# Queries of layer 2's first token group made tile by tile, PSUM banks handed out earlier, and layer 3 put two expert tiles later

## The chip, the core and the metric

The kernel runs on one core of a Trainium2 chip. A core has five engines with a queue of instructions each, and each queue runs in its own order: TensorE (PE; its weight loads are shown apart as PEld), VectorE (DVE), ScalarE (ACT), GpSimd (POOL) and SyncE (SP, which only issues transfers here). The metric is the device time of one execution in microseconds (us), lower is better: 1113.98 us is the median of three runs of the kernel before (1112.86 to 1116.61).

## What is computed

Four layers work on 2048 tokens of width 256 (8 sequences of 256), with a context of 77 rows per sequence. Each layer is a gated cross attention to the context and a gated feed-forward part:

```python
x = x + tanh(g_xattn[i]) * xattn_i(layernorm(x), ctx)
x = x + tanh(g_ffn[i])   * ffn_i(layernorm(x))
```

- Layer 0: attention of 16 heads with exponential features; a product with a sign matrix.
- Layer 1: attention of one head; a feed-forward part 256-1024-256 with ternary weights, activations rounded to 8 bits per token, and GELU.
- Layer 2: attention of 16 heads in which each query keeps only the 64 largest of its 77 scores; a mixture of 8 experts (256-1024-256, GELU), two per token, with a capacity per expert.
- Layer 3: attention of one head with layer norms and a small feed-forward part; a product with a sign matrix, scaled and clipped.

## The kernel before

**Tiles.** Tokens lie in 16 tiles of 128 rows, in 4 groups `X[0]` to `X[3]` of 4 tiles. The residual stream stays in SBUF. A library places the instructions: the program is traced in Python, each instruction gets a priority by its place in the trace (`tc.high_priority(AHEAD)` moves a block up by 1000), and the library decides each engine's order at build time by reckoning when inputs are ready. The order is then fixed. Tiles of a pool with the same tag share a number of buffers (PSUM banks for PSUM pools); a tile takes a free buffer when its turn in the trace comes.

**Layer 1, first group (lines 804 to 811).** A pool of 8 banks is cut in two rings: `chain` (5) serves `cross1(0)` (attention, lines 584 to 611) and `ffns1(0)` (the feed-forward part, two tiles in flight, lines 655 to 700), `beside` (3) serves `cross1(1)`, the attention of group 1, as work on the side. Line 698 is where a tile of layer 1 is done.

**Keys and values of layer 2 (lines 813 to 860).** `kT2` (keys, line 845) and `V2` (values, line 860) come from the context and weights alone. They follow `cross1(1)` in the ring `beside`. After that the pool is closed and its banks are opened anew (lines 999 to 1006): `psm` (3), the score tile `psc` (one buffer of two banks) and `ps` (3).

**Selection of layer 2 (lines 1018 to 1111 and 1383 to 1423).** `queries(0)` normalizes all four tiles of group 0 (`normal_act`, lines 229 to 259), transposes them, multiplies by `wq2` and writes `qT2` with two ACT operations (line 1030). `distances(n)` makes one tile's scores in two halves in `psc` (lines 1047 and 1055), takes the maximum of each head (line 1062) and writes the distances from it to `pr2` (line 1067). `select` then runs two rounds over 16 heads, MAX8 (line 1405) and MATCH_REPLACE8 (line 1417), which strike out the 13 smallest scores. `finish(n)` makes weights from the rest (Abs and Exp on ACT, sum at line 1083, POOL's scaling at line 1085), transposes them (1091), multiplies by `V2` (1097), copies to `oT2` (1103) and projects (1107, 1110).

**Order by hand.** Inside `tc.manual_schedule(engines=ordered)` DVE keeps the order of the trace. `select` calls `gap()` after every 8 heads of a round; each call advances the other work by a step: `front` (`groups1`: layer 1 of groups 1 and 2 with the keys and values of the second half, `keys1`, line 561 to 578), `finish`, `route`, and `queries(g)` of later groups. Whatever a step traces for DVE stands there between the rounds.

**Experts and layer 3 (lines 868 to 984, 1445 to the end).** Routed token rows are gathered from `xbuf`, a tile of 128 at a time, with the weights of the expert (`fetch`, lines 914 and 919, POOL), transposed (930), multiplied (943, GELU 947, 955), scaled (960) and scattered into `ybuf` (965). `experts(0)` has 16 tiles for the first half of the tokens, `experts(1)` 25 for the second half, the last three of them only if needed; the first 8 of these also write rows of the first half. Layer 3's `stream(i)` loads two tiles of results (`yg`, line 1559), adds them (1565), normalizes (1522 to 1530), transposes (1539) and goes on in eight steps. The program traces ten tiles of `experts(1)`, then `run(0, 3)` (three streams), the other expert tiles, then `run(3, 8)`.

Of the kernel before, what the change touches and what calls it, by code (L numbers as in the profile page):

```python
# [21 lines left out]
KC = D // P  # L22
NB = 8
SQ = 256
SK = 77
# [33 lines left out]
def flamingo_kernel(ctx: ExitStack, tc: tile.TileContext, io: dict):  # L59
# [741 lines left out]
    a2s = ExitStack()  # L801
    a2 = a2s.enter_context(tc.tile_pool(name="a2", bufs=1, side="right", reuse_waits="tile"))
    a2w = a2s.enter_context(tc.tile_pool(name="a2w", bufs=2, side="right", reuse_waits="tile"))
    with tc.tile_pool(name="a1p", bufs=8, space=PSUM, side="right", reuse_waits="tile") as ps:
        chain, ps = Banks(ps, "chain", 5), Banks(ps, "beside", 3)
        for _ in cross1(0, chain, b1w, *kv1, False):
            pass
        for _ in ffns1(0, chain, b1w, False):
            pass
        for _ in cross1(1, ps, b1w, *kv1, False):  # L810
            pass

        nm = a2.tile([P, NB, SK], BF16, name="nm")
        nmf = nm.rearrange("p b k -> p (b k)")
        nc.vector.tensor_copy(nmf, mask_u8)
        some = a2.tile([P, NB], F32, name="some")  # L820
        nc.vector.tensor_reduce(some, nm, AX.X, ALU.max)
        nc.vector.tensor_scalar(nmf, nmf, 2.0**100, -(2.0**100), ALU.mult, ALU.add)
        onesb = a2.tile([P, P], BF16, name="onesb")
        nc.vector.memset(onesb, 1.0)
        bq4 = a2.tile([P, KC], F32, name="bq4")
        nc.vector.tensor_scalar(bq4, cols[:, C_WQB * KC : (C_WQB + 1) * KC], 0.25, None, ALU.mult)
        wob3 = rows3(a2, V_WOB, "wob")

        kT2 = a2.tile([P, KC, NB, 2, SK], F32, name="kT2")
        V2 = a2.tile([SK, NB, 8, 2, 2, 16], F32, name="V2")
        nc.gpsimd.memset(V2.rearrange("p b r q s d -> p (b r q s d)"), 0.0)

        for hb in range(2):
            for oc in range(KC):
                pk = ps.tile([P, 512], F32, name="pk", tag="ps")
                for kc in range(KC):
                    nc.tensor.matmul(
                        pk[:, :HB], wk2[:, kc, oc * P : (oc + 1) * P],  # L840
                        ctxT[:, kc, hb * HB : (hb + 1) * HB],
                        start=(kc == 0), stop=(kc == KC - 1),
                    )
                for q in range(2):
                    nc.vector.tensor_scalar(
                        kT2[:, oc, 4 * hb : 4 * hb + 4, q, :],
                        pk[:, :HB].rearrange("p (b k) -> p b k", k=SK),
                        col(C_WKB, oc), par[:, q : q + 1], ALU.add, ALU.mult,
                    )
            for b in range(4 * hb, 4 * hb + 4):  # L850
                pv = ps.tile([P, 512], F32, name="pv", tag="ps")
                for kc in range(KC):
                    nc.tensor.matmul(
                        pv[:SK, :D], ctxT[:, kc, b * SK : (b + 1) * SK], wv2[:, kc, :],
                        start=(kc == 0), stop=(kc == KC - 1),
                    )
                pvv = pv[:SK, :D].rearrange("p (r q d) -> p r q d", q=2, d=16)
                bvv = vrow(V_WVB, SK).rearrange("p (r q d) -> p r q d", q=2, d=16)
                for q in range(2):
                    nc.vector.tensor_add(V2[:, b, :, q, q, :], pvv[:, :, q, :], bvv[:, :, q, :])  # L860


    done1 = [0]
# [43 lines left out]
    def experts(h, psm, f2w, widx, tok, gate, row, ahead=0):  # L907
# [88 lines left out]

    psm = ctx.enter_context(tc.tile_pool(name="f2p", bufs=3, space=PSUM, reuse_waits="tile"))
    banks = ExitStack()  # L1000
    psc = banks.enter_context(
        tc.tile_pool(name="a2s", bufs=1, space=PSUM, side="right", reuse_waits="tile")
    )
    ps = banks.enter_context(
        tc.tile_pool(name="a2p", bufs=3, space=PSUM, side="right", reuse_waits="tile")
    )

    ZR = GT
    zero = work.tile([P, ZR * D], F32, name="zero", tag="xn")
# [6 lines left out]
                )  # L1016

    qs = {}

    def queries(g):  # L1020
        _, xT = normal_act(g, ps)
# [51 lines left out]
    def finish(n, pr):  # L1073

        b = n // 2
        g, t = divmod(n, GT)
        prf = pr.rearrange("p j c k -> p (j c k)")
        nc.scalar.activation(prf, prf, AF.Abs, scale=some[:, b : b + 1])
        nc.scalar.activation(prf, prf, AF.Exp, scale=-1.0)
        yield  # L1080
        yield
        sm = small.tile([P, 4, 4], F32, name="sm")
        nc.vector.tensor_reduce(sm, pr, AX.X, ALU.add)
        nc.vector.reciprocal(sm, sm)  # L1084
        nc.gpsimd.tensor_tensor(pr, pr, sm.unsqueeze(3).to_broadcast([P, 4, 4, SK]), ALU.mult)  # L1085
        po = ps.tile([P, KC, P], F32, name="po", tag="ps")
        for c in range(KC):
            for q in range(2):
                pt = ps.tile([P, 4, P], F32, name="pta", tag="ps")
                for j in range(4):  # L1090
                    nc.tensor.transpose(pt[:SK, j, :], pr[:, j, 2 * c + q, :], ident)  # L1091
                aT = a2w.tile([SK, 4, P], F32, name="aT2", bufs=3)
                nc.scalar.copy(  # L1093
                    aT.rearrange("p j n -> p (j n)"), pt[:SK].rearrange("p j n -> p (j n)")
                )
                for j in range(4):
                    nc.tensor.matmul(  # L1097
                        po[32 * j : 32 * j + 32, c, :],
                        V2[:, b, 4 * c + j, q, :, :].rearrange("p s d -> p (s d)"),
                        aT[:, j, :], start=(q == 0), stop=(q == 1),  # L1100
                    )
        oT = a2w.tile([P, KC, P], F32, name="oT2")
        nc.scalar.copy(oT.rearrange("p c n -> p (c n)"), po.rearrange("p c n -> p (c n)"))
# [289 lines left out]
    def select(n0, n1):  # L1393

        with tc.high_priority(AHEAD):
            for pr in distances(n0):
                nxt = pr
        for n in range(n0, n1):
            pr = nxt
            ahead = distances(n + 1) if n + 1 < n1 else iter(())  # L1400
            rows = [pr[:, j, c, :] for j in range(4) for c in range(4)]
            for r in range(2):
                m8 = a2w.tile([P, H, 8], F32, name=f"m8{r}")
                for i, row in enumerate(rows):
                    nc.vector.max(m8[:, i, :], row)  # L1405
                    if i == H - 1:
                        while n + 1 < n1 and (n + 1) // GT not in qs:
                            gap()
                        with tc.high_priority(AHEAD):
                            nxt = next(ahead, None)  # L1410
                    if i % 8 == 7:
                        gap()
                if r == 1:

                    nc.vector.memset(m8[:, :, NDROP - 8 :], -BIG)
                for i, row in enumerate(rows):
                    nc.vector.match_replace(row, m8[:, i, :], row, -BIG)  # L1417
# [7 lines left out]

    at = {}
    ordered = {mybir.EngineType.DVE}
    with tc.manual_schedule(engines=ordered):
        with tc.high_priority(AHEAD):
            for _ in queries(0):  # L1430
                pass
        front = groups1(psm, kv1)
        steps.append(front)
        select(0, HT)
        last = steps.pop()
        while steps:
            gap()
# [29 lines left out]
    with tc.tile_pool(name="a3", bufs=1, side="right", reuse_waits="tile") as a3, \  # L1467
# [203 lines left out]


        second = experts(1, psm, f2w, *at[1])
        for _ in range(NE + 2):
            next(second)
        n = NT // SN // 2
        run(0, n - 1, [ps])
# [87 lines left out]
```

## Time and profile before

| what | value |
|---|---|
| median of the runs | 1113.98 us |
| the profiled execution's own time | 1120.5 us |
| its span on the chip | 1118.7 us |
| busy: PE, PEld, DVE, ACT, POOL | 906.9, 669.7, 657.7, 495.5, 307.5 us |
| mean granted PE clock | 0.833 of full |
| from 300 to 540 us: DVE busy | 200.9 of 240 us |
| first MAX8 of the selection | 299.77 us |
| first expert tile's matmuls | near 600 us |

The profile is of one execution; its times are microseconds from the start of the span. A row of the timeline has the start, the length, the engine, the line, the operation with output and inputs, how often, and in brackets the idle time of the engine just before with the instruction that ended it. Busy PE is not PE at its peak, since matmuls are pipelined. An idle engine costs something only where the end waits for it.

### The profile page before, as it was taken

To read this page: it belongs to the slowest core of one execution; us is meant where nothing else is said; L and a number is where in the kernel's file an instruction comes from. 1 tells how busy PE (TensorE), PEld (TensorE's weight loads), DVE (VectorE), ACT (ScalarE), POOL (GpSimd) and SP (SyncE) were. 2 spreads that over 40 slices of the span, in tenths; PEclk is the share of its full clock that TensorE was granted. 3 is DMA by queue.
4 is the path that set the end of the run, shared out by engine and by line. 5 is a ranking of instruction groups with operands and counts; after the bars stand their busy time and mean duration, and the time that the engine had idled before them with its cause. 6 is when DMAs were issued, how large, how long until landed. Compare 5 with 4: busy or idle time off the path is not lost.

```text
span 1118.7 us, 16730 instructions
## 1 busy us (share of the span) xinstructions
PE 906.9 (81%) x5884; PEld 669.7 (60%) x5896; DVE 657.7 (59%) x2849; ACT 495.5 (44%) x1012; POOL 307.5 (27%) x333
## 2 busy tenths in 40 slices
PE   4677898958778688686878898899999688997895
PEld 2455565725444345453556776788999676896663
DVE  4779965658588978887677757715300225201664
ACT  3334444124366556564616765543222165222552
POOL 2352323020110300121004223333344363431530
PEclk9689899959967587665557988999999989998697
DMA  6200000003000000100124443566888861782001
GB/s 217 102 1 3 1 1 1 1 1 150 1 0 1 1 1 1 38 1 1 39 81 170 170 169 106 177 238 230 298 304 310 316 216 44 257 322 102 21 11 38
DMA packets 27179, 115.77 MB, mean 103 GB/s; under 512 B 4324, under 2 KB 16332, under 8 KB 21973
## 3 DMA queue, kind: packets, MB, share of 16 engines
q0 software_dynamic: 9504, 90.71, 22.3%
q1 hardware_dynamic: 17589, 23.96, 6.0%
q8 instruction: 48, 0.79, 0.3%
q14 instruction: 38, 0.31, 0.1%
HBM read 99.19 MB, written 15.47 MB: 102 GB/s over the span
## 4 chain that ended last, share of the span: by engine, by line
PE 39%; DVE 22%; ACT 13%; issue 10%; POOL 10%; DMA 5%; SPq 0%; POOLq 0%; ACTq 0%; DVEq 0%
PE pta L1091 3%; PE phm L943 3%; DVE pr L1417 3%; PE pym L955 3%; DMA ybuf<-yo,row 2%; PE pta L473 2%; ACT pr L1067 2%; PE po L1097 2%; DVE m L1405 2%; PE py L488 2%; POOL ybuf L965 2%; DMA yg<-ybuf 2%; POOL xg L914 1%; POOL pr L1085 1%; PE po L476 1%
## 5 line engine op out<-in xcount | busy, mean ns | idle before, releaser
L943 PE MATMUL phm<-xgT,wt 128*128 128x128 f32 x1216 | 152.6, 280 | 1.2 <-ACT yo L960 0.6
L955 PE MATMUL pym<-wt,hT 128*128 128x256 f32 x608 | 149.6, 391 | 3.1 <-ACT hT L947 3.0
L943 PEld LDWEIGHTS phm<-xgT,wt 128*128 128x128 f32 x1216 | 147.5, 195 | 5.8 <-issue 3.0
L955 PEld LDWEIGHTS pym<-wt,hT 128*128 128x128 f32 x608 | 113.7, 195 | 19.2 <-ACT hT L947 4.8
L1417 DVE MATCH_REPLACE8 pr<-m,pr 128x77 f32<-128x77 f32 x512 | 107.1, 224 | 0.0
L1085 POOL TENSOR_TENSOR pr<-pr,sm 128x1232 f32<-128x1232 f32 x16 | 36.0, 2249 | 186.0 <-DVE sm L1084 166.9
L947 ACT ACTIVATE hT<-phm 128x512 f32<-128x512 f32 x76 | 45.4, 597 | 81.6 <-PE phm L943 72.6
L1405 DVE MAX8 m<-pr 128x8 f32<-128x77 f32 x512 | 77.2, 223 | 0.0
L1091 PE MATMUL pta<-ident,pr 128*77 128x128 f32 x256 | 54.4, 351 | 24.2 <-POOL pr L1085 24.2
L1067 ACT ACTIVATE pr<-sc,mx 128x77 f32<-128x77 f32 x256 | 59.0, 340 | 24.8 <-DVE mx L1062 24.7
L919 POOL DMA_INDIRECT wt<-in_w,widx x38 | 37.3, 981 | 111.9 <-PE pym L955 74.8
L1093 ACT COPY aT<-pta 77x512 f32<-77x512 f32 x64 | 36.7, 589 | 63.9 <-PE pta L1091 63.6
L965 POOL DMA_INDIRECT ybuf<-yo,row x46 | 46.2, 1003 | 67.0 <-ACT yo L960 50.5
L1047 PE MATMUL sc<-kT,qT 32*128 32x154 f32 x256 | 38.6, 406 | 31.1 <-ACT pr L1067 30.9
L1565 DVE TENSOR_TENSOR x<-x,yg 128x512 f32<-128x512 f32 x16 | 12.8, 807 | 86.6 <-DMA yg<-ybuf 86.5
L960 ACT ACTIVATE yo<-pym,gate 128x256 f32<-128x256 f32 x38 | 18.1, 476 | 98.6 <-issue 48.9
L1091 PEld LDWEIGHTS pta<-ident,pr 128*77 128x77 f32 x256 | 37.8, 189 | 38.7 <-POOL pr L1085 26.8
L474 ACT COPY aT<-pta 77x512 f32<-77x512 f32 x64 | 35.5, 581 | 56.4 <-PE pta L473 56.4
L456 POOL TENSOR_TENSOR pr<-pr,sm 128x1232 f32<-128x1232 f32 x16 | 36.8, 2300 | 84.7 <-DVE sm L455 50.1
L914 POOL DMA_INDIRECT xg<-xbuf,tok x38 | 37.5, 986 | 74.2 <-PE ptm L930 50.2
L473 PE MATMUL pta<-ident,pr 128*77 128x128 f32 x256 | 44.8, 319 | 16.0 <-POOL pr L456 9.2
L1047 PEld LDWEIGHTS sc<-kT,qT 32*128 32x128 f32 x256 | 25.1, 239 | 45.4 <-ACT pr L1067 38.3
(387 smaller groups left out, 1944.8 us busy)
## 6 DMA issues: line engine op xcount, KB each, us to landing
ybuf<-zero SPq DMA_DIRECT2D x8, 512.0 KB
yg<-ybuf SPq DMA_DIRECT2D x16, 256.0 KB
xbuf<-xn SPq DMA_DIRECT2D x6, 512.0 KB
x<-in_x SPq DMA_DIRECT2D x4, 512.0 KB
raw_f1w<-in_f1w SPq DMA_DIRECT2D x2, 1024.0 KB
out<-x SPq DMA_DIRECT2D x8, 256.0 KB
vec<-in_vec SPq DMA_DIRECT2D x1, 896.0 KB
ybuf<-yo,row POOLq DMA_INDIRECT x46
```

Of the source, the lines that this page charges most:

```text
L473: nc.tensor.transpose(pt[:SK, j, :], pn2[i][:, j, c, :], ident)
L914: nc.gpsimd.indirect_dma_start(out=xg[:, :], out_offset=None, in_=xbuf[h][:, :], in_offset=bass.IndirectOffsetOnAxis(ap=tok[:, m : m + 1], ...
L943: nc.tensor.matmul(ph[:, i, :], wt[:, kc * FF + fc * P : kc * FF + (fc + 1) * P], xgT[:, kc, :], start=(kc == 0), stop=(kc == KC - 1),)
L947: nc.scalar.activation(hT[:, NFC // 2 * fq : NFC // 2 * (fq + 1), :], ph, AF.Gelu)
L955: nc.tensor.matmul(py, hT[:, fc, :], wt[:, KC * FF + fc * D : KC * FF + (fc + 1) * D], start=(fc == 0), stop=(fc == NFC - 1),)
L965: nc.gpsimd.indirect_dma_start(out=dst[:, :], out_offset=bass.IndirectOffsetOnAxis(ap=row[:, m : m + 1], axis=0), in_=yo[:, :], in_offset= ...
L1047: nc.tensor.matmul(sc[:, jj, c * 2 * SK : (c + 1) * 2 * SK], qT[32 * j : 32 * j + 32, c, t * P : (t + 1) * P], kT2[32 * j : 32 * j + 32, c ...
L1067: nc.scalar.activation(pr[:, j0 + jj, c, :], sc[:, jj, c * SK : (c + 1) * SK], AF.Identity, bias=mx[:, jj, c : c + 1], scale=-1.0,)
L1085: nc.gpsimd.tensor_tensor(pr, pr, sm.unsqueeze(3).to_broadcast([P, 4, 4, SK]), ALU.mult)
L1091: nc.tensor.transpose(pt[:SK, j, :], pr[:, j, 2 * c + q, :], ident)
L1405: nc.vector.max(m8[:, i, :], row)
L1417: nc.vector.match_replace(row, m8[:, i, :], row, -BIG)
```

## The change

Four edits.

1. **Banks.** The pools `psm`, `psc` and `ps` are opened at the start of layer 1, ahead of `cross1(0)`, and the pool of 8 with its two rings is gone. `cross1(0)` and `ffns1(0)` take from `psm` (3 banks), the side work from `ps` (3).
2. **Side work.** The keys `kT2` of both halves now come ahead of `cross1(1)` in the trace; the values `V2` stay behind it.
3. **Queries.** `queries(0)` is replaced by `queries0(t)` for each tile: statistics on DVE, four small operations on POOL, one normalizing ACT operation, two transposes and four matmuls in a tile of `psc`, three more ACT operations. Its two SBUF tiles share the two buffers of `oT2`. Tile 0 is traced ahead of the ordered part, tile 1 ahead of the first round, and tile n+2 behind the first MAX8 of the second round of selection n.
4. **Layer 3.** `run(0, 3)` is traced behind twelve tiles of `experts(1)`, not ten.

```diff
-    with tc.tile_pool(name="a1p", bufs=8, space=PSUM, side="right", reuse_waits="tile") as ps:
-        chain, ps = Banks(ps, "chain", 5), Banks(ps, "beside", 3)
-        for _ in cross1(0, chain, b1w, *kv1, False):
-            pass
-        for _ in ffns1(0, chain, b1w, False):
-            pass
-        for _ in cross1(1, ps, b1w, *kv1, False):
-            pass
+    psm = ctx.enter_context(tc.tile_pool(name="f2p", bufs=3, space=PSUM, reuse_waits="tile"))
+    banks = ExitStack()
+    psc = banks.enter_context(
+        tc.tile_pool(name="a2s", bufs=1, space=PSUM, side="right", reuse_waits="tile")
+    )
+    ps = banks.enter_context(
+        tc.tile_pool(name="a2p", bufs=3, space=PSUM, side="right", reuse_waits="tile")
+    )
+    for _ in cross1(0, psm, b1w, *kv1, False):
+        pass
+    for _ in ffns1(0, psm, b1w, False):
+        pass
...
+    for hb in range(2):
+        for oc in range(KC):
+            pk = ps.tile([P, 512], F32, name="pk", tag="ps")
...
+    for _ in cross1(1, ps, b1w, *kv1, False):
+        pass
+    for b in range(NB):
+        pv = ps.tile([P, 512], F32, name="pv", tag="ps")
...
+    def queries0(t):
+
+        if t == 0:
+            qs[0] = a2w.tile([P, KC, GN], F32, name="qT2")
+        x, rows = X[0][:, t, :], slice(t * P, (t + 1) * P)
+        xn = a2w.tile([P, D], F32, name="xn_q0", tag="oT2")
+        xT = a2w.tile([P, KC, P], F32, name="xT_q0", tag="oT2")
+        st = small.tile([P, 6], F32, name="q0_st")
+        mv = small.tile([P, 2], F32, name="q0_mv")
+        nc.vector.bn_stats(st, x)
+        nc.vector.bn_aggr(mv, st)
+        rs = small.tile([P, 1], F32, name="q0_rs")
+        nc.gpsimd.tensor_scalar(rs, mv[:, 1:2], EPS, None, ALU.add)
+        nc.gpsimd.tensor_tensor(rs, rs, mhalf[:, :1], ALU.pow)
+        m = small.tile([P, 1], F32, name="q0_nm")
+        nc.gpsimd.tensor_tensor(m, mv[:, 0:1], rs, ALU.mult)
+        nc.gpsimd.tensor_scalar(m, m, -1.0, None, ALU.mult)
+        nc.scalar.activation(xn, x, AF.Identity, bias=m, scale=rs)
+
+        two = psc.tile([P, 2, 512], F32, name="sc")
+        pt, pq = two[:, 0, : KC * P], two[:, 1, : KC * P]
+        for kc in range(KC):
+            nc.tensor.transpose(
+                pt[:, kc * P : (kc + 1) * P], xn[:, kc * P : (kc + 1) * P], ident
+            )
+        nc.scalar.copy(xT, pt.rearrange("p (c n) -> p c n", c=KC))
+        for oc in range(KC):
+            for kc in range(KC):
+                nc.tensor.matmul(
+                    pq[:, oc * P : (oc + 1) * P], wq2[:, kc, oc * P : (oc + 1) * P],
+                    xT[:, kc, :], start=(kc == 0), stop=(kc == KC - 1),
+                )
+            nc.scalar.activation(
+                qs[0][:, oc, rows], pq[:, oc * P : (oc + 1) * P], AF.Identity,
+                bias=bq4[:, oc : oc + 1], scale=0.25,
+            )
...
-        oT = a2w.tile([P, KC, P], F32, name="oT2")
+        oT = a2w.tile([P, KC, P], F32, name="oT2", tag="oT2")
...
+            if n == 0:
+                with tc.high_priority(AHEAD):
+                    queries0(1)
             for r in range(2):
                 m8 = a2w.tile([P, H, 8], F32, name=f"m8{r}")
                 for i, row in enumerate(rows):
                     nc.vector.max(m8[:, i, :], row)
+                    if r == 1 and i == 0 and n + 2 < GT:
+                        with tc.high_priority(AHEAD):
+                            queries0(n + 2)
...
+    with tc.high_priority(AHEAD):
+        queries0(0)
     with tc.manual_schedule(engines=ordered):
-        with tc.high_priority(AHEAD):
-            for _ in queries(0):
-                pass
...
-        for _ in range(NE + 2):
+        for _ in range(NE + 4):
             next(second)
```

More of the change, by code (lines that the diff above doesn't have):

```diff
@@ L803, in flamingo_kernel @@
     a2w = a2s.enter_context(tc.tile_pool(name="a2w", bufs=2, side="right", reuse_waits="tile"))
-    with tc.tile_pool(name="a1p", bufs=8, space=PSUM, side="right", reuse_waits="tile") as ps:
-        chain, ps = Banks(ps, "chain", 5), Banks(ps, "beside", 3)
-        for _ in cross1(0, chain, b1w, *kv1, False):
-            pass
-        for _ in ffns1(0, chain, b1w, False):
-            pass
-        for _ in cross1(1, ps, b1w, *kv1, False):
-            pass
[L817 to L860, printed above, removed]
@@ new lines, in flamingo_kernel @@
+    psm = ctx.enter_context(tc.tile_pool(name="f2p", bufs=3, space=PSUM, reuse_waits="tile"))
[10 more added lines that the diff above has]
+        pass
+    nm = a2.tile([P, NB, SK], BF16, name="nm")
@@ new lines, in flamingo_kernel @@
+    nmf = nm.rearrange("p b k -> p (b k)")
+    nc.vector.tensor_copy(nmf, mask_u8)
+    some = a2.tile([P, NB], F32, name="some")
+    nc.vector.tensor_reduce(some, nm, AX.X, ALU.max)
+    nc.vector.tensor_scalar(nmf, nmf, 2.0**100, -(2.0**100), ALU.mult, ALU.add)
+    onesb = a2.tile([P, P], BF16, name="onesb")
+    nc.vector.memset(onesb, 1.0)
+    bq4 = a2.tile([P, KC], F32, name="bq4")
+    nc.vector.tensor_scalar(bq4, cols[:, C_WQB * KC : (C_WQB + 1) * KC], 0.25, None, ALU.mult)
+    wob3 = rows3(a2, V_WOB, "wob")
@@ new lines, in flamingo_kernel @@
+    kT2 = a2.tile([P, KC, NB, 2, SK], F32, name="kT2")
+    V2 = a2.tile([SK, NB, 8, 2, 2, 16], F32, name="V2")
+    nc.gpsimd.memset(V2.rearrange("p b r q s d -> p (b r q s d)"), 0.0)
+    for hb in range(2):
[3 more added lines that the diff above has]
+                nc.tensor.matmul(
+                    pk[:, :HB], wk2[:, kc, oc * P : (oc + 1) * P],
+                    ctxT[:, kc, hb * HB : (hb + 1) * HB],
+                    start=(kc == 0), stop=(kc == KC - 1),
+                )
+            for q in range(2):
+                nc.vector.tensor_scalar(
+                    kT2[:, oc, 4 * hb : 4 * hb + 4, q, :],
+                    pk[:, :HB].rearrange("p (b k) -> p b k", k=SK),
+                    col(C_WKB, oc), par[:, q : q + 1], ALU.add, ALU.mult,
+                )
@@ new lines, in flamingo_kernel @@
+    for _ in cross1(1, ps, b1w, *kv1, False):
[3 more added lines that the diff above has]
+        for kc in range(KC):
+            nc.tensor.matmul(
+                pv[:SK, :D], ctxT[:, kc, b * SK : (b + 1) * SK], wv2[:, kc, :],
+                start=(kc == 0), stop=(kc == KC - 1),
+            )
+        pvv = pv[:SK, :D].rearrange("p (r q d) -> p r q d", q=2, d=16)
+        bvv = vrow(V_WVB, SK).rearrange("p (r q d) -> p r q d", q=2, d=16)
+        for q in range(2):
+            nc.vector.tensor_add(V2[:, b, :, q, q, :], pvv[:, :, q, :], bvv[:, :, q, :])
@@ L986, in experts @@
                     one(m, NM[h])
[L999 to L1006, printed above, removed]
     ZR = GT
@@ L1018, in flamingo_kernel @@
     qs = {}
+    def queries0(t):
[17 more added lines that the diff above has]
+        pt, pq = two[:, 0, : KC * P], two[:, 1, : KC * P]
+        for kc in range(KC):
+            nc.tensor.transpose(
+                pt[:, kc * P : (kc + 1) * P], xn[:, kc * P : (kc + 1) * P], ident
+            )
+        nc.scalar.copy(xT, pt.rearrange("p (c n) -> p c n", c=KC))
+        for oc in range(KC):
+            for kc in range(KC):
+                nc.tensor.matmul(
+                    pq[:, oc * P : (oc + 1) * P], wq2[:, kc, oc * P : (oc + 1) * P],
+                    xT[:, kc, :], start=(kc == 0), stop=(kc == KC - 1),
+                )
+            nc.scalar.activation(
+                qs[0][:, oc, rows], pq[:, oc * P : (oc + 1) * P], AF.Identity,
+                bias=bq4[:, oc : oc + 1], scale=0.25,
+            )
     def queries(g):
```

## Prediction

> **What bounds the kernel now.** I read the table of stretches first, then who waited for whom, then the instructions in order of time at the two places that the change touches. The page's own chain is spread thin (PE 39%, DVE 22%, ACT 13%, issue 10%), so shares do not help: each place has its own limit.
>
> Around 300 us layer 1 hands over to layer 2. Columns: stretch, length, busy us of PE, PEld, DVE, ACT, POOL, then PE clock, DMA share, GB/s.
>
> ```profile
> 236.00:260.00 24.00, 15.07 (x68) 7.64 (x70) 18.98 (x64) 8.01 (x12) 6.07 (x6) 0.66 0.34 139
> 260.00:272.00 12.00, 8.78 (x50) 5.02 (x49) 7.08 (x20) 7.70 (x11) 0.00 (x0) 0.86 0.18 72
> 272.00:288.00 16.00, 15.11 (x81) 10.48 (x80) 13.16 (x40) 4.37 (x8) 1.71 (x4) 1.00 0.01 2
> 288.00:300.00 12.00, 12.00 (x60) 6.72 (x60) 1.75 (x4) 5.05 (x15) 0.00 (x0) 1.00 0.00 0
> ```
>
> From 272 to 300 PE is full (27.1 of 28 us) and DVE, which will carry the selection, does 1.75 us of work in the last 12. The DVE rows say why:
>
> ```profile
> 260.20 0.47 DVE L698 SCALAR_TENSOR_TENSOR x<-pyf,q_dn,x 128x256 f32<-128x256 f32 x1
> ...
> 280.05 0.48 DVE L698 SCALAR_TENSOR_TENSOR x<-pyf,q_dn,x 128x256 f32<-128x256 f32 x1 [0.61 <-PE pyf L693]
> ...
> 294.84 0.80 DVE L1062 TENSOR_REDUCE mx<-sc 128x8 f32<-128x616 f32 x1 [7.06 <-PE sc L1055]
> 299.05 0.80 DVE L1062 TENSOR_REDUCE mx<-sc 128x8 f32<-128x616 f32 x1 [3.41 <-PE sc L1055]
> 299.77 1.21 DVE L1405 MAX8 m<-pr 128x8 f32<-128x77 f32 x8
> 300.90 1.27 DVE L578 TENSOR_TENSOR V<-pv,vec 77x512 f32<-77x512 f32 x2
> ```
>
> Tile 0 of group 0 leaves layer 1 at 260.7, tile 3 at 280.5; the first MAX8 comes at 299.77, because the queries are made for the four tiles at once. Right behind stands L578, layer 1's values for the second half: in the order written for DVE it precedes the rest of the first selection.
>
> From 780 to 885 PE is full with expert tiles, one each 7.24 us (L943 starts at 844.19 and 851.43). There it stops:
>
> ```profile
> 885.42 1.46 PE L955 MATMUL pym<-wt,hT 128*128 128x256 f32 x6
> 887.93 0.69 DVE L1565 TENSOR_TENSOR x<-x,yg 128x512 f32<-128x512 f32 x1 [80.61 <-DMA yg<-ybuf]
> ...
> 898.98 2.08 ACT L1530 ACTIVATE xn<-x,n_nm,n_rs 128x256 f32<-128x256 f32 x4 [12.98 <-DVE n_nm L1528]
> 899.63 1.39 PE L1539 MATMUL pt<-ident,xn 128*128 128x128 f32 x4 [12.75 <-ACT xn L1530]
> 900.82 2.77 PE L955 MATMUL pym<-wt,hT 128*128 128x256 f32 x6
> ```
>
> Layer 3's first transposes stand in PE's order inside the eleventh expert tile (6 of its 16 pym are out), and their input needs the scatters of tile 8, a load and a normalization: PE stands 12.75 us with work behind it.
>
> **Banks and kT2.** Five banks become three for group 0's layer 1. Its tiles take banks in program order: ptx of tile 2 (259.96) follows pyf of tile 0 (259.09) although five are there. Gelu empties a bank in 0.7 us. I take 0, bounds 0 and +3. kT2 now stands ahead of cross1(1) in its ring. Before, its first matmul came at 272.46, just behind the last pyv of cross1(1) (271.75), although PE idled 8.9 us in 236:260. It can now fill 218:236, where PE idles 6.4 us and DVE 11.5: 16 matmuls, 4.6 us of PE (L839), and 8 DVE operations of 0.54 (4.3 us) leave the full stretch. Pushed between the links of cross1(0), each is at most 0.59 long: +1 us, bounds 0 and +2.
>
> **Queries by tile.** One tile's chain: statistics 0.42 + 0.17; POOL four small ones, 1.96 us for four columns (281.37 to 283.33), the power 1.04 of it (0.71 for two columns, L1526), so 1.5; ACT xn 0.59; two transposes 0.4; ACT copy 0.37 (L932); four matmuls 0.9; the last ACT 0.39 (between 0.34 for 77 columns and 0.465 for 256). With hand-overs 6 us, 7 to the first mx. For group 0, eight short query activations replace two of 0.69: ACT +1.7 us, in a stretch where it is 5 to 8 of 12 us busy; at nothing, or 1.7 if that cover goes. Tile 0: 260.7 + 6 = 266.7; from complete queries to the first MAX8 the rows take 5.8 (293.97 to 299.77); with 2 for a crowded ACT, MAX8 at 275. DVE then does eight and waits for L578. That is PE's matter: from 272 to 300 it loses 4.6 (kT2) and 4.7 (queries: eight L1026 at 0.43, transposes 1.2), and gains 1.3 (tile 1), net 8, and values of layer 2 may use the 3.2 us idle in 260:272. L578 comes at 290 to 293: **-10** us, bounds -5 (kT2 alone) and -13.
>
> **What the new waits take back.** The shared score tile has one buffer, and queries0 takes it too. Tile 2's chain stands in DVE's order behind the first MAX8 of the second half; the next mx on it came 2.9 us after that point (314.5 to 317.33). 7 + 0.6 against 2.9: DVE stands 4.5 us, and all select and front work is queued behind that mx. The next idle on DVE, 3.35 at 326.69 waiting for gelu, is then partly over: +2 net, bounds 0 and +4.5. Tile 1's chain costs 1 at most, inside L578's wait. Tile 3's is worse: its two tiles share the two slots of oT2, and in program order oT of tile 0 stands ahead.
>
> ```profile
> 339.26 1.42 DVE L1083 TENSOR_REDUCE sm<-pr 128x16 f32<-128x1232 f32 x1
> 349.74 0.78 DVE L1062 TENSOR_REDUCE mx<-sc 128x8 f32<-128x616 f32 x1
> 356.30 0.41 ACT L1103 COPY oT<-po 128x256 f32<-128x256 f32 x1
> ```
>
> oT came 17.0 us behind sm, the mx 10.5. Now: oT at sm + 15.4 (the 1.8 us of L1067 just ahead of it go behind), then xn to mx, 4.4: mx at sm + 19.8, a stall of 9.3. The idles that follow (1.60, 1.39, 1.22 at 352 to 363) are absorbed: **+5**, bounds 0 and +17. Over the eight tiles sm to oT takes 12.6 to 23.5; the last gives the upper end (23.5 + 4.4 - 10.5). No DMA moves past another one here, and V2's memset and the zeroing keep their cover. Sum of this half: +1 - 10 + 2 + 5 = -2.
>
> **Layer 3 two tiles later.** Ten expert tiles ahead become twelve. PE's place for the transposes moves from 886.9 to behind the rest of the eleventh tile (10 x 0.226 = 2.3) and the twelfth (7.24): 896.4. Their input is ready at 899.6 as before; 3.2 us of 12.75 stay: **-9.5**. Bounds: 0, if the transposes still slip in early; -14, with the whole wait and the 1.4 us of the slow restart (below) gone. POOL changes too: the thirteenth tile's fetches now come ahead of layer 3 in the program. Before, they went out at 896.95 and 900.24, behind n_rs, which waited 9.13 us; if they stay there, PE has after 899.6 only layer 3's serial work until those weights land, and the gain shrinks towards its lower end. The streams end near 960 and twelve tiles of 7.24 followed; with ten left they are still covered, so the tail does not move.
>
> The restart is slow in the rows: six pym take 2.77 us at 900.82 and 1.36 at the pace of the tiles before (16 in 3.62), 1.4 apart, at a PE clock of 0.55 in 899.6:905 and 1.00 after. I count none of it. [...]
>
> **Sum.** -2 - 9.5 = -11.5. The profiled execution took 1120.5 us (span 1118.7, 1.8 around it), 6.5 above the median 1113.98; the differences are carried to the median: 1102.5.
>
> **Rivals.**
> 1. Forecast: start pulled forward, mostly eaten by the query waits; layer 3's wait mostly gone: 1102.5, chance 0.50.
> 2. The waits are absorbed by idle that comes anyway (DVE idles 39 us in 300:540): +1 - 10 - 9.5 = -18.5, 1095.5. For: each later idle waits for ACT or PE, which run on. Against: the select order is serial. 0.15.
> 3. Layer 3 does not move: the planner put the transposes where its own reckoning had the input ready, mid-tile, and may again find a hole there. -2: 1112. 0.17.
> 4. Slower. The oT2 ring: place, the third selection's second mx; price, 17.4 at the longest sm to oT, with 4.5 and 1 before it and nothing absorbed, 23. It decides once the stalls pass the 10 + 9.5 gained, less 1 for kT2. 23 + 1 - 19.5 = +4.5: 1118.5. For: every DVE instruction there is in a written order. Against: with DVE standing, ACT and PE reach oT sooner. 0.15.
>
> The other 0.03 is for causes not listed: 0.01 near no change, 0.02 slower.
>
> **Numbers.** 0.3% is 3.3 us, about what a measurement of this kernel tells from none. Faster: 0.50 + 0.15 + 0.05 of rival 3 = 0.70. Within: its other 0.12 and 0.01, 0.13. Slower: 0.15 and 0.02, 0.17. The range 1091 to 1117 takes in the forecast with its bounds, rival 2 and rival 3, and leaves out most of rival 4.
>
> **What would show it.** Right: first MAX8 near 275; L578 near 291; an idle of some 9 us on DVE ahead of an mx, ended by PE sc, about 20 us after the first sm; kT2 before 236; the L1539 wait down to about 3 and standing behind the twelfth pym. Wrong: L578 still at 300, no idle at those mx, L1539 inside the eleventh tile, or the first expert tile starting as late as now.

## The result, and the profile after

The changed kernel took 1124.1 us (median of 12 runs, 1118.3 to 1126.6) and the one before, beside it, 1117.19 (12 runs, 1112.86 to 1121.1): ratio 1.0057, interval 1.0038 to 1.0075. The forecast of 1102.5 and its range of 1091 to 1117 miss it.

Two later sets gave the same kernel 0.9979 (0.9952 to 1.0005) and 0.9971 (0.9949 to 0.9993). So the sign is not settled; what is settled is that the 11.5 us of the forecast are not there. The profiles say why, if they are cut at five landmarks, A, C, D, E and F (there is no B). All numbers are us; "again" and "third" are profiled executions of the two later sets, one each.

| stretch | before | after | again | third |
|---|---|---|---|---|
| start to A: the last sixteen matmuls of L303 (layer 0) begin | 214.5 | 219.4 | 218.6 | 220.2 |
| A to C: fourth L698 of group 1, layer 1 | 152.8 | 160.4 | 158.8 | 160.5 |
| C to D: first expert matmul | 229.6 | 228.6 | 228.7 | 226.5 |
| D to E: layer 3's first load is issued | 276.9 | 273.0 | 269.2 | 272.4 |
| E to F: last expert scatter | 149.5 | 148.4 | 146.4 | 147.9 |
| F to the end of the span | 95.4 | 94.0 | 94.9 | 94.2 |
| A to the end | 904.2 | 904.4 | 897.9 | 901.5 |

**The first row is not the change's.** The edits begin behind A: on PE, DVE, ACT and POOL both programs run the same instructions in the same order until 5.5 us behind it. Yet of the 20 profiled executions in this study 7 reached A at 213.9 to 214.6 and 13 at 218.3 to 222.3. The table of stretches shows where, before first, then after (same columns as in the prediction):

```profile
75.00:80.00 5.00, 4.33 (x36) 2.48 (x34) 3.79 (x7) 3.36 (x5) 2.25 (x1) 1.00 0.00 0
85.00:90.00 5.00, 3.38 (x36) 2.04 (x35) 4.96 (x6) 1.58 (x3) 0.00 (x0) 1.00 0.06 12
```

```profile
75.00:80.00 5.00, 4.33 (x24) 2.65 (x20) 2.59 (x5) 2.70 (x4) 1.45 (x1) 0.50 0.00 0
85.00:90.00 5.00, 5.00 (x23) 4.06 (x24) 4.56 (x4) 0.00 (x0) 1.09 (x1) 0.50 0.00 0
```

With the same idle of 4.1 us on PE near 68 (4.10 and 4.09) the granted clock falls to half (0.50 from 70 to 75 in both); in one execution it is back at 75, in the other at 90. So 4.9 us must be taken off every later time of the changed kernel's first profile before it is set beside the old one. Below, "A + 56" means 56 us behind A.

**The start.** Stretches of the changed kernel and DVE's rows:

```profile
272.00:288.00 16.00, 13.37 (x91) 8.94 (x93) 11.66 (x37) 8.86 (x27) 2.15 (x4) 0.92 0.01 2
288.00:300.00 12.00, 12.00 (x69) 8.49 (x69) 4.22 (x15) 2.30 (x4) 0.00 (x0) 1.00 0.00 0
```

```profile
265.12 0.47 DVE L698 SCALAR_TENSOR_TENSOR x<-pyf,q_dn,x 128x256 f32<-128x256 f32 x1
...
285.41 1.07 DVE L1443 MAX8 m<-pr 128x8 f32<-128x77 f32 x7
...
290.97 0.48 DVE L698 SCALAR_TENSOR_TENSOR x<-pyf,q_dn,x 128x256 f32<-128x256 f32 x1 [1.28 <-PE pyf L693]
...
299.09 0.69 DVE L578 TENSOR_TENSOR V<-pv,vec 77x512 f32<-77x512 f32 x1 [3.32 <-PE pv L574]
```

PE is full in the last 12 us, as it was. These windows are not moved by the 4.9 us: in the same place behind A (283.09 to 295.09) DVE was busy for 3.95 of 12 us before, so its 4.22 us are hardly more. Tile 0 is done at A + 45.7, as before. The first MAX8 comes at A + 66.0 (before: 85.3), 19 us sooner. But L578, behind which the rest waits, comes at A + 79.7 against 86.4: 6.7 sooner. Tile 3 is done at A + 71.6 against 65.5.

**The two waits.** Below, "mx" is the reduction that takes the maximum of each head (two for each tile), and "sm" the sum in `finish`. The fourth mx came without a wait before:

```profile
317.33 0.78 DVE L1062 TENSOR_REDUCE mx<-sc 128x8 f32<-128x616 f32 x1
```

Now tile 2's queries are made ahead of it. On the engines that they pass through:

```profile
314.00 0.41 DVE L1027 BATCH_NORM_STATS2 q_st<-x 128x6 f32<-128x256 f32 x1
315.64 4.41 PE L592 MATMUL pq<-xT,w_wq 128*128 128x512 f32 x6 [0.46 <-ACT xT L258]
316.31 0.60 ACT L1035 ACTIVATE xn_q<-x,q_nm,q_rs 128x256 f32<-128x256 f32 x1 [0.23 <-POOL q_nm L1034]
319.89 0.38 PE L1040 MATMUL sc<-ident,xn_q 128*128 128x128 f32 x2
325.03 0.80 DVE L1097 TENSOR_REDUCE mx<-sc 128x8 f32<-128x616 f32 x1 [7.72 <-PE sc L1090]
```

The normalized tile is there at 316.9, but PE's order has six matmuls of layer 1's queries in front, and the transposes start at 319.89. PE's granted clock was 0.50 from 313 to 318 us, and the first four of the six start 0.85 to 1.0 us apart, the last two 0.43. Layer 1's matmuls stand between the later steps of the chain too (320.20 to 321.56, 322.00 to 322.85). The mx stands 7.72 us. Tile 3's:

```profile
343.44 1.42 DVE L1118 TENSOR_REDUCE sm<-pr 128x16 f32<-128x1232 f32 x1
347.39 0.41 DVE L1027 BATCH_NORM_STATS2 q_st<-x 128x6 f32<-128x256 f32 x1
357.84 0.38 ACT L1138 COPY oT<-po 128x256 f32<-128x256 f32 x1
358.11 0.61 ACT L1035 ACTIVATE xn_q<-x,q_nm,q_rs 128x256 f32<-128x256 f32 x1
363.08 0.80 DVE L1097 TENSOR_REDUCE mx<-sc 128x8 f32<-128x616 f32 x1 [9.06 <-PE sc L1090]
```

Its statistics are taken at 347.39 and its normalization runs at 358.11, right behind oT, whose ring it shares. The mx comes 19.6 us behind sm and stands 9.06.

**Layer 3.** The issue of the loads (SP), first before, then after, and the root of the first streams before (POOL):

```profile
873.85 11.78 SPq L1559 DMA_DIRECT2D yg<-ybuf  x6
...
898.01 2.06 POOL L1526 TENSOR_TENSOR n_rs<-n_rs,mhalf 128x2 f32<-128x2 f32 x3
```

```profile
881.39 12.64 SPq L1599 DMA_DIRECT2D yg<-ybuf  x6
```

After, the loads as they land (DVE), the root (POOL), and PE:

```profile
904.16 0.69 DVE L1605 TENSOR_TENSOR x<-x,yg 128x512 f32<-128x512 f32 x1 [7.74 <-DMA yg<-ybuf]
907.09 0.23 POOL L1565 TENSOR_SCALAR n_rs<-n_mv 128x2 f32<-128x2 f32 x1
...
918.54 2.06 POOL L1566 TENSOR_TENSOR n_rs<-n_rs,mhalf 128x2 f32<-128x2 f32 x3
...
920.16 1.39 PE L1579 MATMUL pt<-ident,xn 128*128 128x128 f32 x4 [9.89 <-ACT xn L1570]
```

The first stream's additions are done at 904.9 and its epsilon is added at 907.09. But POOL takes its power (the first of the three at 918.54) only behind the epsilon additions of the second and third stream (915.13 and 917.12), and these wait for their own loads. The order was the same before (the three powers in a row from 898.01, behind the last epsilon at 896.58); there the loads landed closer together. PE stands 9.89 us, in the thirteenth tile, with the input 38.8 us behind the loads' issue (881.39) instead of 25.8 (873.85 to 899.63).

### The profile page after: what moved, and what is told of

It is laid out like the page before. It is cut to its first block, busy times and chain, and to the rows that moved or that the text cites. A ratio compares the mean times of both kernels' runs of the same rounds, so it can differ in the third digit from the quotient of the medians.

```text
span 1123.8 us, 16790 instructions
## 1 busy us (share of the span) xinstructions
PE 906.2 (81%) x5907; PEld 670.9 (60%) x5920; DVE 657.1 (58%) x2849; ACT 497.3 (44%) x1020; POOL 310.6 (28%) x345
## 4 chain that ended last, share of the span: by engine, by line
PE 39%; DVE 24%; ACT 12%; POOL 10%; issue 9%; DMA 6%; SPq 1%; POOLq 0%; ACTq 0%; DVEq 0%
PE pta L1126 3%; DVE pr L1458 3%; DMA yg<-ybuf 3%; PE phm L949 3%; PE py L488 2%; DVE m L1443 2%; DMA ybuf<-yo,row 2%; PE po L1132 2%; PE pym L961 2%; PE pta L473 2%; ACT pr L1102 2%; POOL ybuf L971 2%; POOL pr L1120 2%; DVE sm L1118 2%; PE sc L1082 1%
## 5 line engine op out<-in xcount | busy, mean ns | idle before, releaser
L961 PE MATMUL pym<-wt,hT 128*128 128x256 f32 x608 | 146.8, 386 | 3.0 <-ACT hT L953 3.0
L1126 PEld LDWEIGHTS pta<-ident,pr 128*77 128x77 f32 x256 | 37.7, 189 | 39.1 <-POOL pr L1120 26.6
L473 PEld LDWEIGHTS pta<-ident,pr 128*77 128x77 f32 x256 | 33.4, 170 | 31.0 <-issue 12.7
```

Source lines behind the costliest of these rows:

```text
L473: nc.tensor.transpose(pt[:SK, j, :], pn2[i][:, j, c, :], ident)
L961: nc.tensor.matmul(py, hT[:, fc, :], wt[:, KC * FF + fc * D : KC * FF + (fc + 1) * D], start=(fc == 0), stop=(fc == NFC - 1),)
```

## Experiments

Three theories are open. T1: the waits for the queries of tiles 2 and 3 eat the earlier start. T2: layer 3's input came later with the tiles, so its wait moved instead of going. T3, the rival: the loss sits ahead of A and is chance. Ratios are to the runs of before in the same set.

**Each part alone, and the whole again.** Layer 3 alone is the kernel before with

```diff
-        for _ in range(NE + 2):
+        for _ in range(NE + 4):
```

> The kernel before with twelve expert tiles ahead of layer 3 instead of ten, nothing else. Theory A (the loads of layer 3 share the DMA engines with two more tiles' weights, so their input is later too, and PE's wait moves instead of going): PE still waits about 10 us ahead of the first transposes, the yg loads land over some 15 us instead of 6, gain about 3 us, ratio 0.995 to 0.999. Theory B (the term of the prediction: input ready as before, wait down to 3): ratio 0.990 to 0.993. Theory C (the whole loss of the change comes from here): slower, ratio 1.004 or more.

Ratio 0.999 (0.9969 to 1.001), not told apart from no gain. Theory A is right about the place: PE's wait is 6.74 (it had about 10), E to F 144.7 against 149.5. The eight additions of loaded rows run from 887.2 to 912.5 (before: 887.9 to 895.7); the first stream's are done at 889.2, and its power comes at 914.74. The start alone is the changed kernel with NE + 2:

> The changed kernel with ten tiles ahead of layer 3, so the part at the start of layer 2 alone. Theory A (the two query chains that the selection waits for cost more than the earlier start brings): idles on DVE of about 7.7 and 9 us ahead of the mx of the second and third selection; from the last L303 matmuls of layer 0 to the fourth L698 of group 1 about 160 us against 152.8 before; time 5 to 10 us above before, ratio 1.004 to 1.009. Rival (the 4.9 us by which the profiled execution is late already at 215 us are all there is, and they are the changed program's own): the lateness at 215 us comes again, and the stretch behind it costs about nothing. Rival C: the start part is worth nothing and layer 3 loses, ratio 0.999 to 1.001.

Ratio 1.000 (0.9977 to 1.0022); waits 7.69 and 9.06, A to C 160.3. This execution reached A at 214.0 with the changed start: the lateness of 4.9 does not belong to it. Theory A's waits and stretch are there, but not its 1.004 to 1.009; what becomes of the difference is told at the end of the next section.

> The changed kernel itself once more, beside the same runs of before as the other kernels of this set. Since its two parts alone came out at 1.000 and 0.999, theory A (the two parts add up, and the first ratio of 1.0057 held several us of the executions' own scatter, which comes from the clock granted between 70 and 90 us) expects 0.998 to 1.001. Theory B (the two parts together cost something that neither costs alone): 1.004 to 1.008. In either case the stretch from the last L303 matmuls to the fourth L698 of group 1 is 160 to 161 us again.

0.9979 (0.9952 to 1.0005).

> The changed kernel a third time. If the first ratio of 1.0057 was its worth: 1.003 to 1.008. If it held the scatter of executions: 0.996 to 1.001, as the second time.

0.9971 (0.9949 to 0.9993). Both ratios lie just below the 0.998 to 1.001 of theory A of the former, and theory B is out: the parts add up to about nothing. The stretch of 160 to 161 came out at 158.8 and 160.5. The changed kernel's medians in its three sets are 1124.1, 1120.8 and 1121.6, those of before in six sets 1117.2, 1124.1, 1122.9, 1123.6, 1123.2 and 1121.0. It is the first set's before that stands out, so T3 holds for the sign of the first ratio, as far as this goes: whether chance or the chip of that set made it is not shown.

**The waits (T1).** All three other tiles' queries right behind the first distances:

```diff
             if n == 0:
                 with tc.high_priority(AHEAD):
-                    queries0(1)
+                    for q in range(1, GT):
+                        queries0(q)
...
-                    if r == 1 and i == 0 and n + 2 < GT:
-                        with tc.high_priority(AHEAD):
-                            queries0(n + 2)
```

> Start part alone, but the queries of tiles 1, 2 and 3 are all written right behind the first tile's distances, ahead of the first MAX8; nothing of them stands behind a MAX8 or behind the first oT any more. Theory A (the waits are the loss): no idle over 3 us ahead of an mx in 300 to 370, the stretch from the last L303 to the fourth L698 of group 1 is 146 to 150 us, time 3 to 8 us below before, ratio 0.993 to 0.998. Rival (PE is full from 285 to 300, and what is made earlier there delays L578 by as much): the waits are gone but L578 is 4 to 6 us later than in the start part alone, ratio 0.998 to 1.002.

Ratio 0.9926 (0.9901 to 0.9951). The same two mx as above, fourth (319.63) and sixth of the selection, stand for nothing:

```profile
351.79 0.78 DVE L1097 TENSOR_REDUCE mx<-sc 128x8 f32<-128x616 f32 x1
```

A to C is 151.4, 8.9 less than in the start alone, and the ratio is 0.0074 lower, 8.3 us: what the waits cost reaches the end, which is T1. The rival is half right, L578 comes 4.1 us later (A + 83.7), and the stretch is 1 us longer than theory A had it. A whole selection ahead instead of half of one (`r == 0` in the hook):

> Start part alone, with each tile's queries a whole selection ahead instead of half of one: tile 2's behind the first MAX8 of the first selection, tile 3's behind the first MAX8 of the second, which is ahead of the first oT in the program. Theory A: both waits fall under 2 us, since the 8 to 16 us of the chains then have 20 us ahead of them; ratio 0.993 to 0.998, as with all three at first. Rival (the shared score tile with one buffer is the cause, wherever the chain stands): a wait of 5 us or more moves to the mx of the first selection's second half, ratio 1.000 to 1.005.

Ratio 1.0001 (0.9977 to 1.0025), A to C 155.7. Theory A fails here, the rival holds up to the place: tile 2's wait is gone, tile 3's has moved to the fifth mx, by the shared score tile.

```profile
340.61 0.80 DVE L1097 TENSOR_REDUCE mx<-sc 128x8 f32<-128x616 f32 x1 [8.25 <-PE sc L1090]
```

Same places, but a bank of `ps` instead of the score tile:

```diff
-        two = psc.tile([P, 2, 512], F32, name="sc")
-        pt, pq = two[:, 0, : KC * P], two[:, 1, : KC * P]
+        two = ps.tile([P, 2, KC * P], F32, name="pq0", tag="ps")
+        pt, pq = two[:, 0, :], two[:, 1, :]
```

> Start part alone, where the queries take a bank of the ring of three instead of the one score tile; written at the same places. Theory A (the third mx of the selection stands because the score tile is taken by tile 2's queries): the wait of 7.7 us at the fourth mx goes to under 1, and the selection that needs those queries comes half a selection later with the chain ready; the wait for tile 3's queries ahead of the sixth mx goes too, and what is left of it stands at the next mx. Stretch from the last L303 to the fourth L698 of group 1: 148 to 155 us. Rival (the chain of 8 to 14 us is simply too long for the place, whatever it is held in): the waits move on by one mx and keep 5 us or more each, stretch 157 to 161.

Ratio 0.9996 (0.9962 to 1.0031), A to C 154.7. No wait from the fourth to the eighth mx, as theory A has it (the third has 2.20). But tile 0's queries now come later (first mx with 3.24 idle), MAX8 at A + 82.4, L578 at A + 83.5: the early start is given away at the front.

**kT2 and the banks.** kT2's block put back behind `cross1(1)`:

> Start part alone, with the sixteen kT2 matmuls and their eight DVE operations put back behind the cross attention of group 1, as before. The prediction's term: kT2 ahead costs at most 1 us in the front and takes 4.6 us off the full stretch, so L578 comes 4 to 5 us later than in the start part alone (84 to 85 us behind the last L303 against 79.6). Rival (PE is not what L578 waits for, or the matmuls ahead push layer 1 back as much as they bring): L578 within 1.5 us of 79.6, and the first L698 earlier than 45.7.

Ratio 1.0122 (1.0074 to 1.0169, 2 runs). L578 at A + 84.0, 4.4 later: the prediction's term. The tile 0 of layer 1 is not earlier (46.2). What was not foreseen is that the two waits grow to 8.91 and 13.36 and A to C to 171.2. The banks alone, in the kernel before:

```diff
-        chain, ps = Banks(ps, "chain", 5), Banks(ps, "beside", 3)
+        chain, ps = Banks(ps, "chain", 3), Banks(ps, "beside", 3)
```

> The kernel before with three banks instead of five for the chain of group 0's layer 1 and nothing else. The prediction's term: nothing, bounds 0 and +3; the four L698 at 45.7, 53.3, 59.9 and 65.5 us behind the last L303 as before. Rival (the later tiles 1 to 3 of the changed kernel, 57.0, 63.0 and 71.5, come from the banks): the same lateness of 3 to 6 us shows here without any queries.

Ratio 1.000 (0.9976 to 1.0025). The tiles are done at A + 46.5, 54.3, 64.7 and 70.4. The first two are 0.8 and 1.0 late, the others 4.8 and 4.9; but the jump comes with the clock, first before, then three banks:

```profile
270.00:274.00 4.00, 4.00 (x27) 2.58 (x27) 2.62 (x7) 2.31 (x3) 0.00 (x0) 1.00 0.00 0
```

```profile
270.00:274.00 4.00, 4.00 (x13) 1.09 (x13) 1.12 (x4) 1.01 (x2) 0.00 (x0) 0.50 0.00 0
```

PE is full in both, with 27 matmuls and with 13. So the banks themselves cost about 1; whether they also brought the clock down, one execution cannot say.

**Layer 3 (T2).** What holds the first stream, its loads or the order? First the epsilon on VectorE, so that POOL has only the powers, with ten and with twelve tiles:

```diff
-            nc.gpsimd.tensor_scalar(rs, mv[:, :, 1], eps, None, ALU.add)
+            nc.vector.tensor_scalar(rs, mv[:, :, 1], eps, None, ALU.add)
```

> The kernel before, ten tiles ahead of layer 3, with one edit in layer 3's normalization: the variance's epsilon is added on VectorE instead of GpSimd. GpSimd's order then no longer holds the first stream's power behind the epsilon additions of the second and third stream. Theory A (the first transposes wait for the third stream's loads, by GpSimd's order, and not only for their own): PE's wait of 12.75 falls to 6 to 8, 4 to 6 us below before, ratio 0.994 to 0.997. Rival (the loads of all three land together, or the fetches that stand behind the powers are late next): the wait falls but PE waits as long a few us later, ratio 0.999 to 1.001.

Ratio 0.9983 (0.9965 to 1.0001), the wait 11.0: theory A's number fails. The multiplication by the mean (L1528, 899.58) now stands on DVE behind all eight additions, of which the last starts at 898.72; another order holds the same thing.

> The same edit with twelve tiles ahead of layer 3. Theory A (two things held layer 3 up after the move: its loads on DMA engines that also fetch two more tiles' weights, and the power behind the third stream's data): the first stream's input is ready about 1 us before or after the end of the twelfth tile, the wait is 0 to 2 us, ratio 0.989 to 0.993, so the prediction's -9.5 is found only here. Rival (only the DMA engines count): the wait stays at 8 or more, ratio 0.996 to 0.999.

Ratio 0.9956 (0.9933 to 0.9978), wait 7.93, E to F 143.8: far from theory A's wait of 0 to 2 and just below the rival's numbers. The same edit with the three queries at first:

> The start part with the three other tiles' queries at first, and the epsilon on VectorE; ten tiles ahead. If the parts add up: 0.9926 less 0.004 to 0.006, so 0.987 to 0.989. If the scatter of executions made the 0.9926: 0.992 to 0.996.

> The same with twelve tiles ahead of layer 3. If the parts add up: 0.981 to 0.986, the fastest of all here. Rival (twelve tiles bring nothing once the power is free, since the fetches of the tiles behind stand in GpSimd's order behind the powers of later streams): as with ten, within 0.002 of it.

0.9926 (0.9899 to 0.9952) with ten tiles and 0.9904 (0.9878 to 0.993) with twelve: with ten the epsilon adds nothing, and the sums forecast were too low. Then DVE's order in layer 3 as the streams are written, each one's normalization ahead of the next one's additions:

```diff
+        with tc.manual_schedule(engines=ordered):
             run(0, n - 1, [ps])
             for _ in second:
                 pass
             run(n - 1, 2 * n, [ps, psm])
```

> The kernel before with twelve tiles ahead of layer 3 and VectorE's order in layer 3 kept as the streams are written, so that the first stream's normalization stands ahead of the additions of the second and third. Theory A (order: the first stream's own data are there about 7 us before its transposes start): PE's wait is 0 to 3, ratio 0.989 to 0.994. Theory B (DMA engines: the first stream's own second load lands 15 to 20 us after its issue with two more tiles fetched, too late whatever the order): the wait is 4 to 8, ratio 0.995 to 0.998. Rival C (the written order makes VectorE stand later in layer 3, where streams overlap): the wait goes but the tail behind the last scatter grows from 94 to 98 us or more.

> The same written order with ten tiles. Theory A: the wait falls from 12.75 to 5 to 8, since the first stream's data were there at 891.7 and its transposes started at 899.6; ratio 0.994 to 0.997. Theory B: the wait stays above 10, ratio 0.998 to 1.001.

> The changed kernel with the three other tiles' queries at first and layer 3 in the written order, twelve tiles ahead. If the parts add up: 0.9926 less 0.004 to 0.010, so 0.983 to 0.989, faster than before and than the changed kernel. If the written order costs in the tail: 0.990 to 0.996.

Ratios 1.0328 (1.0296 to 1.036), 1.0365 (1.0323 to 1.0406) and 1.0285 (1.0248 to 1.0323). The wait is 7.86 with ten tiles and 0.16 with twelve, and E to F falls to 133.8 with twelve: theory A for the wait. But F to the end grows to 142.9, 146.6 and 146.7, beyond what rival C had asked for: eight streams in one written order on DVE wait for each other. So the order only for the three streams beside expert tiles and the first step of the fourth (`run` yields once a step):

```diff
+        with tc.manual_schedule(engines=ordered):
+            for _ in run(0, n - 1, [ps]):
+                pass
             for _ in second:
                 pass
+            tail = run(n - 1, 2 * n, [ps, psm])
+            next(tail)
+        for _ in tail:
+            pass
```

> The kernel before with twelve tiles ahead of layer 3; VectorE's order is the written one for the first three streams and the first part of the fourth alone. Theory A (the wait was an order on VectorE and GpSimd, the price lay in the later streams): PE's wait 0 to 2, last scatter 133 to 137 us after the first load's issue, tail behind it 94 to 99, time 9 to 14 us below before, ratio 0.987 to 0.992. Rival (the first streams' own written order costs as much behind them): tail 104 or more, ratio 0.998 or more.

Ratio 0.9937 (0.9887 to 0.9986); E to F 137.8, F to the end 99.7, each just beyond theory A's numbers and short of the rival's. The first stream's root and PE:

```profile
900.86 0.74 POOL L1526 TENSOR_TENSOR n_rs<-n_rs,mhalf 128x2 f32<-128x2 f32 x1
...
902.49 0.33 PE L1539 MATMUL pt<-ident,xn 128*128 128x128 f32 x1
```

So it was for the most part the order that held the first stream, which bears out T2. The power is taken for one stream (x1), 8 us behind the addition of its second load (892.71) instead of 14, and PE comes without a wait. That addition came 18.5 us behind the loads' issue, between before's 15.8 and the changed kernel's 22.8. With the three queries at first:

> The changed kernel with the three other tiles' queries at first and the same written order in layer 3. If the parts add up: 0.9926 less 0.008 to 0.013, so 0.979 to 0.985, the fastest here. Rival as for the other: 0.990 to 0.993.

1109.13 us against 1121.03 (6 and 11 runs), ratio 0.9893 (0.9852 to 0.9935); E to F 133.9, F to the end 101.3. Above the sum expected, but faster than both kernels, and not told apart from the epsilon version with twelve tiles (0.9904).

## Why the prediction was wrong, step by step

- **Banks, 0 with bounds 0 and +3.** About right: 0.8 to 1.0 at tiles 0 and 1 in the run with three banks. The 4 more behind a half clock are not settled.
- **kT2, +1 and 4.6 off the full stretch.** Right: tile 0 of the changed kernel is not late at all, and L578 moves by 4.4. (The 272.46 that the prediction gives for the first matmul is its weight load; the matmul starts at 272.67.)
- **The start, -10.** Mis-sized: -6.7 at L578, within its bounds. MAX8 was forecast 60.5 behind A and came at 66.0. The step that failed is the list of what PE has in the full stretch. It counted what tile 1's queries take out and not that tile 0's, let in front by priority, cut up tile 1's last matmuls (272.29 to 275.83 on PE), and that layer 1's own tiles 1 to 3 then come 3.7, 3.1 and 6.1 us later, into it; PE also stood 2.13 us ahead of tile 1's transposes (285.68). Of the 5.5 us that the MAX8 is late, 4 lie between the second mx (280.64) and it: DVE does layer 1's operations and those of the values there, where before 0.7 us passed.
- **Tile 2's wait, 4.5 gross, +2 net.** Mis-sized: 7.72 gross. Against before, DVE went from 5.6 early at the third mx to 2.8 late at the fourth, and was 0.7 early again at the fifth: +4.8 net, just beyond the bound of +4.5. The chain of 7 had no place for six of layer 1's matmuls ahead of it on PE.
- **Tile 3's wait, 9.3 gross, +5 net.** The mechanism and the size were right (19.6 us from sm to mx, 19.8 forecast; 9.06 of wait). What failed is "the idles that follow are absorbed": of the three idles named, the 1.60 is gone, but the two that end with PE are still there with 2.20 and 1.22 us (1.39 and 1.22 before). DVE is 8.4 late at the sixth mx, 7.6 at the seventh and at the eighth. Net +8.3.
- **The sum of this half, -2.** Measured +7.6 at C. Rival 4 had named the place; its mechanism was there, at 13.1 us net instead of 23.
- **Layer 3, -9.5.** The failed step: "their input is ready at 899.6 as before". Behind the loads' issue it was ready at 38.8 us instead of 25.8. PE's place was mis-sized too, the other way: the transposes again stand inside a tile, the thirteenth, as rival 3 had feared, and PE reached them 28.9 us behind the loads' issue instead of 13.0, which is 15.9 later where the sum had 9.5. With the input as before, no wait would have been left. Two more tiles' weights are fetched in the meantime (DMA share 15 to 30 us behind the issue 0.98, before 0.35; in the first 15 us 0.97 and 0.99), the eight additions spread over 20.6 us and, with layer 3 alone, 25.3 instead of 7.8, and the engines' orders make the first stream wait for the last. The written order shows that these orders are the lever; that the fetches spread the loads is read from the rows and not shown by a run that leaves them out. With the planner's order E to F was 148.0 to 150.8 in seven executions with ten tiles (mean 149.93) and 144.7 to 148.4 in four with twelve (146.85): 3.1 us gained.
- **The bound of 0.3%.** It is too tight for one set of this kernel: the same two programs gave 1.0057 and 0.9971, which the intervals within a set do not hold. The two lengths of the half clock ahead of A (to 75 and to 90 us in the two profiles, with A 4.9 us apart) are large enough for it; that they were unevenly spread in the first set was not measured.
- **The slow restart, counted as none.** A wait as short as the 3.2 us forecast did not come about in the changed kernel: six pym behind the 9.89 us took 2.77, as before, at a granted clock of 0.50 from 918 to 925 us. With the written order and twelve tiles, where the wait is 0.16, the clock stays at 1.00 (900 to 930 us) and six pym take 1.50.

Still open: +7.6 at C and -3 in E to F would leave +4.6, and the ratios of the later sets lie below 1. In the first pair of profiles the changed kernel wins back 1.0 from C to D, 3.9 from D to E, 1.0 from E to F and 1.4 behind F, so that A to the end is the same to 0.2. D to E is 3.4 us shorter over all profiles (means of 276.3 in eight executions with before's start and 272.9 in twelve with the changed one), but it goes with the clock granted in it, whichever start the kernel has:

| mean granted clock, D to E | executions (before's start, changed start) | D to E, us |
|---|---|---|
| 0.99 | 0, 3 | 268.8 to 271.0 |
| 0.96 to 0.97 | 2, 7 | 272.3 to 274.3 |
| 0.95 | 6, 2 | 275.5 to 278.1 |

Whether the changed start brings the higher clock, or few executions happened to have it, was not tried.

## What to carry to other kernels

Where a chain is put half a step ahead, count what stands in front of it on each engine it passes and what must be free before it may start, and take a wait in a written order as lost: here, of 16.8 us of waits 3.5 came back before the next one and 0.9 behind them. Before work is moved past a stall, ask whether the stalled input arrives at a fixed time or moves along; here loads and an engine's order moved it, from 25.8 to 38.8 us behind the loads' issue. A planner's order that takes several streams' data for ready at once makes the first wait for the last: look at which other stream's rows stand between a stream's data and its next step.

## What was not expected of the hardware

The half clock that came with one and the same idle of 4.1 us lasted 5 us behind it in the profiled execution of before (0.50 from 70 to 75 us, 1.00 from 75) and about 21 in that of the changed kernel (0.50 from 70 to 90 us, 0.99 from 90 to 95), with PE busy 4.3 to 5.0 of every 5 us of it. No run here shows why.
